# An attention block with mixture of experts: program order for the first weights and tokens, and the experts' gathers, scatters and row scalings in other slots

## The chip, the core and the metric

The kernel runs on one core of a Trainium2 chip. TensorE (PE in the profile, PEld for its weight loads) multiplies, VectorE (DVE), ScalarE (ACT) and GpSimd (POOL) do elementwise work, SyncE (SP) issues most DMAs, and POOL issues the indirect ones (gather and scatter by a list of row numbers). Every engine works through its own queue in the program's order. The metric is device time of one execution in microseconds (us); less is better. Before the change the median of three runs is 1076.01 us (1075.66 to 1076.06).

## The reference

The input is x, 2 batches of 1024 tokens with 512 features. The block is attention with a residual and a layer norm, then a mixture of experts with a residual and a layer norm:

```python
q, k, v = (lora_linear(x, W, b, Bm, Am) for each of q, k, v)   # x W^T + b + 0.5 (x Bm^T) Am^T
attn = softmax(q k^T / sqrt(32))                               # 16 heads of 32
x = layernorm(x + lora_linear(attn v, Wo, bo, Bo, Ao))
probs = softmax(x @ Wg)                                        # 8 experts, top 1
pos = position of the token in its expert's list; keep = pos < 256
h = silu(xd[e] @ W1[e]) * (xd[e] @ W3[e])                      # xd[e]: the 256 rows of expert e, H = 704
oe = h @ W2[e]
out = oe[row of the token] * gate * keep
shared = silu(x @ sw1) * (x @ sw3) @ sw2
x = layernorm(x + out + shared)
```

## The kernel before

**Precision.** A matrix operand is kept as two tiles, a rounded high part and the rest, low (wh and wl, xh and xl, hs with two halves, w13s and w2s with two halves). A product is three matmuls: high by high, low by high, high by low. ACT casts the high half, DVE or POOL subtracts to make the low half.

**The start (lines 341 to 361).** SP loads, in this order: the two LoRA factors of the Q weight, then weight chunk 0, x chunk 0, weight chunk 1, x chunk 1, up to chunk 3 (`load_w(0, ...)` with `load_xk` in its loop), then the two LoRA factors and four chunks of the K weight (`load_w(1)`). PE warms up with four matmuls on a zeroed tile (`hot`, L349). `fold_w` (L251 to L266) splits the LoRA factors and multiplies them into PSUM (`lp`, L264). For each chunk k, `split_w` adds `lp` to the raw weight (L270, DVE), casts the high part (`wh`, L271, ACT) and subtracts the low part (`wl`, L272, DVE); `split_xk` casts `xh` (L282, ACT) and subtracts `xl` (L283, POOL for the first token block); `proj_k` (L297) then runs twelve matmuls, three for each of four head groups, which need `xh` and `wh`, then `xl` and `wh`, then `xh` and `wl`. Between chunks 1 and 2 of the Q projection stands the preparation of the K weight (`prep_w(1, r1)`). In this stage PE's order is written out by hand (`manual_schedule(engines=MAN1)`, MAN1 is PE alone); the order on ACT, DVE and POOL is made by the framework's scheduler. The two memsets of L361 stand last in the code, and the scheduler puts one of them at the front of POOL's queue and one behind the four `xl`.

**Attention** follows, and then the shared expert, in eight blocks of 256 tokens. The router scatters the rows with their gate and token number into an HBM tensor by expert (`xd_d`), and the shared result plus residual goes to HBM as `bs_d`.

**The experts (lines 1090 to 1143).** One expert e has 256 rows and six slots c = 0 to 5, one for each chunk of 128 of the hidden width (chunk 5 is 64 wide). The order on PE, and from here on on ACT, DVE, POOL and SP too (MAN3 and MAN4), is the program's. A slot holds: `ffn1` (24 matmuls into one of three PSUM banks `hp`, 12 in slot 5, L829), `glu` (silu on ACT, L840, and product on DVE, L841), a load of a w13 chunk five ahead (L503), `w2_load` (L807), the high and low halves of the next expert's w13 chunk (L511 on ACT, L517 on DVE), and `split_h` (hs, L849 on ACT and L850 on DVE). The PSUM bank is free when both halves of hs are made. Beside this:

- Slot 1 of expert e holds `expert_out` of expert e - 1, for both halves of 128 rows: 17 matmuls each (`y`, L873), which take hs and w2s chunk by chunk, chunk 5 last; DVE then adds the gated result to the row's base (`be`, L1036) and takes the row statistics (L531 to L534).
- Slot 3 holds `prep_expert` of the next expert (eight transposes on PE, L413; high and low halves, L416 and L417).
- `w2_split(e, q)` makes w2s chunk q: ACT casts (L816), POOL subtracts (L817). The table `W2_AT` says in which slot: chunks 0 and 1 in slot 2, chunk 2 in slot 3, chunk 3 in slot 4, chunks 4 and 5 in slot 5. The raw tiles w2r have four buffers; the load of the tile four chunks on follows a slot after the split that frees its buffer.
- `load_base(j)` (L1023) gathers the base rows of half j from `bs_d` by an indirect DMA on POOL into a tile `be` with four buffers. Half 2e is gathered in slot 3 of expert e, half 2e + 1 in slot 5.
- For the two halves of expert e - 1: `norm_root` in slot 2 (POOL: a power, L540, and a small product, L542), `norm_rows_act` in slot 3 (ACT scales the rows, L546), `store_out` in slots 4 and 5 (POOL, indirect DMA to the output, L1040).

After expert 7 its own output, statistics, scaling and scatter close the kernel.

Of the kernel before, what the change touches and what calls it, by code (L numbers as in the profile page):

```python
# [9 lines left out]
F32 = mybir.dt.float32  # L10
# [8 lines left out]
P = 128  # L19
# [4 lines left out]
NG = 4  # L24
KC = D // P
R = 16
LR = 64 + R
LORA = 0.5
SCALE = HD ** -0.5
E, CAP, H = 8, 256, 704  # L30
# [5 lines left out]
WARM, WCOL = 4, 256  # L36
# [7 lines left out]
}  # L44
MAN1 = {mybir.EngineType.PE}
MAN2 = {
    mybir.EngineType.PE, mybir.EngineType.Activation, mybir.EngineType.DVE,
    mybir.EngineType.Pool, mybir.EngineType.SP,
# [14 lines left out]
BTB = 4  # L63
AHEAD = 5
W2_END = {2: (0, 1, 2), 3: (3, 4), 4: (5,)}
W2_AT = {2: (0, 1), 3: (2,), 4: (3,), 5: (4, 5)}
MPJ, MPP = 0, 2
RDIR = NU - 2
FINE, NRME = 2, 4
# [23 lines left out]
def kernel(  # L93
# [5 lines left out]
    def f(ap):  # L99
        return ap.bitcast(F32)  # L100
# [112 lines left out]
    with ExitStack() as ph1, tc.manual_schedule(engines=MAN1):  # L213
# [4 lines left out]
        def bank1(nm):  # L218
            if next(turn) == 3:
                return avp.tile([P, 512], F32, name=nm, tag="av")  # L220
            return one.tile([P, 512], F32, name=nm, tag="one")
# [7 lines left out]
        wl = [wp.tile([P, KC, D], F32R, name=f"wl{i}") for i in range(3)] + [wo_l]  # L229
        bv_bc = wp.tile([P, D], F32, name="bv_bc")  # L230

        def load_w(i, also=lambda k: None):
            raws = []
            for j in range(2):
                raw = next(lraw_s)[0:LR]
                sp.dma_start(out=raw, in_=lora[i, j])
                raws.append(raw)
            for k in range(KC):
                raw = next(wraw_s)
                sp.dma_start(out=raw, in_=wT[i, k])  # L240
                raws.append(raw)
                also(k)
            return raws


        def prep_w(i, raws):
            for k, lp in enumerate(fold_w(i, raws)):
                split_w(i, k, raws, lp)

        def fold_w(i, raws):  # L250
            ba = []  # L251
            for j, lo in ((0, 64), (1, 32)):
                t_ = sg.tile([LR, D], F32R, name=f"lora{i}{j}", tag=f"lora{j}", bufs=1)
                act.copy(t_, raws[j])
                rows = slice(lo, lo + R)
                dve.tensor_tensor(t_[rows], raws[j][rows], f(t_[rows]), ALU.subtract)
                ba.append(t_)
            lps = []
            for k in range(KC):
                if k == KC - 1:  # L260
                    lp = avp.tile([P, 512], F32, name=f"lp{i}{k}", tag="av")
                else:
                    lp = s1p.tile([P, 512], F32, name=f"lp{i}{k}", tag="s1")
                pe.matmul(lp, ba[0][:, k * P : k * P + P], ba[1], start=True, stop=True)  # L264
                lps.append(lp)
            return lps  # L266

        def split_w(i, k, raws, lp):
            raw = raws[2 + k]
            dve.scalar_tensor_tensor(raw, lp, LORA, raw, ALU.mult, ALU.add)  # L270
            act.copy(wh[i][:, k, :], raw)  # L271
            dve.tensor_tensor(wl[i][:, k, :], raw, f(wh[i][:, k, :]), ALU.subtract)  # L272

        def load_xk(tb, k):
            raw = next(xraw_s)
            sp.dma_start(out=raw, in_=xT[tb, k])
            return raw

        def split_xk(tb, k, raw):
            hi = sg.tile([P, 512], F32R, name=f"xh{tb}{k}", tag="xh", bufs=6)  # L280
            lo = sg.tile([P, 512], F32R, name=f"xl{tb}{k}", tag="xl", bufs=6)
            act.copy(hi, raw)  # L282
            (pool if tb == 0 else dve).tensor_tensor(lo, raw, f(hi), ALU.subtract)  # L283
            return hi, lo
# [7 lines left out]
        def proj_k(o, xs, w, g, k):  # L292
            hi, lo = xs[k]
            a = wh[w][:, k, g * P : g * P + P]
            c = wl[w][:, k, g * P : g * P + P]
            for i, (lhs, rhs) in enumerate(((a, hi), (a, lo), (c, hi))):
                pe.matmul(o, lhs, rhs, start=k + i == 0, stop=k + i == KC + 1)  # L297
# [36 lines left out]
        def pre_s1(tb):  # L334
            if tb == 3:
                for i in pre:
                    s1_step(i // 2, i % 2 * 2)
                    s1_step(i // 2, i % 2 * 2 + 1)
                    break

        x0 = []
        r0 = load_w(0, lambda k: x0.append(load_xk(0, k)))
        r1 = load_w(1)
        sp.dma_start(out=bqk_sb, in_=bqk)

        dve.memset(bo_bc, 0.0)
        for i in range(WARM):
            hot = one.tile([P, 512], F32, name=f"hot{i}", tag="one")
            pe.matmul(hot[:, 0:WCOL], bo_bc[:, 0:P], bo_bc[:, 0:WCOL], start=True, stop=True)  # L349
        lps = fold_w(0, r0)  # L350
        os_ = [bank1(f"o00{g}") for g in range(NG)]
        xs = []
        for k in range(KC):
            split_w(0, k, r0, lps[k])
            xs.append(split_xk(0, k, x0[k]))
            for g in range(NG):
                proj_k(os_[g], xs, 0, g, k)
            if k == KC - 3:
                prep_w(1, r1)
        for k_ in Ks:  # L360
            pool.memset(f(k_[96:98, :, :]), -1.0)  # L361
        for tb in range(4):
            if tb == 0:
                for g in range(NG):
# [445 lines left out]
    def w2_split(e, c):  # L810
        raw = wraw[e, 6 + c]
        if e == E - 1 and c < 2:
            hl = po["frw"].tile([P, 2, 2, 512], F32R, name=f"w2t{c}", tag="w13s", bufs=6)[:, 0]
        else:
            hl = fr.tile([P, 2, 512], F32R, name=f"w2s{e}_{c}", tag="w2s", bufs=6)
        act.copy(hl[:, 0, :], raw)  # L816
        pool.tensor_tensor(hl[:, 1, :], raw, f(hl[:, 0, :]), ALU.subtract)  # L817
        wchunk[e, 6 + c] = hl
# [202 lines left out]
    def load_base(j):  # L1021
        bases[j] = fr.tile([P, D], F32, name=f"be{j}", tag="bt", bufs=BTB)
        pool.indirect_dma_start(  # L1023
            out=bases[j],
            out_offset=None,
            in_=bs_d,
            in_offset=bass.IndirectOffsetOnAxis(ap=meta[:, j, 1:2].bitcast(I32), axis=0),
        )
# [10 lines left out]
    def store_out(j):  # L1039
        st_ = pool.indirect_dma_start(  # L1040
            out=out,
            out_offset=bass.IndirectOffsetOnAxis(ap=meta[:, j, 1:2].bitcast(I32), axis=0),
            in_=bases[j],
            in_offset=None,
        )
        st_ = st_.ins
        tc.declare_no_dep(st_, group="out", reason="different rows")
        tc.add_to_no_dep_group("out", st_)
# [41 lines left out]
    with tc.manual_schedule(engines=MAN4):  # L1090
        last = None
        for e in range(E):
            nxt = e + 1
            hss = []
            for c in range(6):
                for q in W2_END.get(c, ()) if nxt == E else ():
                    w2_split(e, q)
                hp = ffn1(e, 0, xte[e], c)
                glu(e, 0, c, hp)
                n = nxt * 6 + c  # L1100
                if n + AHEAD < E * 6:
# [12 lines left out]
                if nxt < E:  # L1114
                    w13_low(nxt, c)
                if c == 1:
                    if e:
                        for hf in range(2):
                            expert_out(e - 1, last, hf)
                    else:  # L1120
                        pend()
                if c == 3 and nxt < E:
                    prep_expert(nxt)
                if c in (3, 5):
                    load_base(2 * e + c // 2 - 1)
                for q in W2_AT.get(c, ()) if nxt < E else ():
                    w2_split(e, q)
                if e:
                    for hf in range(2):
                        j = 2 * (e - 1) + hf  # L1130
                        if c == 2:
                            norm_root(outs[j])
                        if c == 3:
                            norm_rows_act(bases[j], bases[j], outs[j])
                        if c == 4 + hf:
                            store_out(j)
            last = hss
        for hf in range(2):
            j = 2 * (E - 1) + hf
            expert_out(E - 1, last, hf)  # L1140
            norm_root(outs[j])
            norm_rows_act(bases[j], bases[j], outs[j])
            store_out(j)
# [61 lines left out]
```

## Time and profile before

| what | value |
|---|---|
| median of three runs | 1076.01 us |
| the profiled execution, its own time | 1076.59 us |
| its span, first to last instruction | 1074.9 us |
| PE busy | 1038.9 us, 97% of the span |
| DVE / ACT / POOL busy | 748.3 / 530.1 / 573.1 us |
| mean granted TensorE clock | 0.993 of full |
| data moved by DMA | 131.24 MB |

The span leaves 1.7 us of the execution's time outside. A row of a timeline has the start, the duration, engine, line, operation, what it writes and reads, and in brackets the idle time of the engine before it with what ended it; a row with x2 or more is a merged run, whose duration reaches from the first start to the last end. A row of the sums by stretch has the length, then busy time and count for PE, PEld, DVE, ACT and POOL, then the granted clock, the share of time in which the 16 DMA engines were busy, and GB/s. Ends of matmuls are modelled; starts are measured, so distances between starts are used.

### The profile page before, as it was taken

The numbers are of one execution on the slowest core, as the hardware profiler recorded it, in microseconds if no ns is written. First come the engines' busy times: TensorE is split into PE (matmuls) and PEld (weight loads), VectorE is DVE, ScalarE is ACT, GpSimd is POOL, SyncE is SP. The second block draws the span as 40 slices with busy tenths as digits, with TensorE's granted clock in tenths as the row PEclk, the third lists the DMA queues.
The fourth block names the chain that finished last, engine by engine and source line by source line (L and its number), as shares of the span: only waits on it lengthen the run. The fifth ranks groups of instructions, "written<-read, shape, count | busy, mean of one in ns | idle before, by whom it ended". The sixth has DMA issues, their size and how long they took to land. (4 is left out here: it accounts for less than half of the span.)

```text
span 1074.9 us, 16446 instructions
## 1 busy us (share of the span) xinstructions
PE 1038.9 (97%) x5992; PEld 742.9 (69%) x5992; DVE 748.3 (70%) x1217; ACT 530.1 (49%) x1026; POOL 573.1 (53%) x379
## 2 busy tenths in 40 slices
PE   8999999999999999999999999999999999999996
PEld 6888774444444455544444369889999998888885
DVE  6732788999999987799998784233522556777762
ACT  5422215666666655556666756222222455555552
POOL 5000007888888877868899575000050045666674
PEclk8999999999999999999999999999999999999999
DMA  8866860141414242042520123000082556777731
GB/s 279 288 219 202 252 195 25 52 110 48 103 47 106 71 109 70 22 90 70 119 81 22 51 60 109 20 21 20 31 240 95 161 184 207 234 234 235 237 107 59
DMA packets 77585, 131.24 MB, mean 122 GB/s; under 512 B 14344, under 2 KB 23048, under 8 KB 77504
## 3 DMA queue, kind: packets, MB, share of 16 engines
q1 hardware_dynamic: 73664, 117.59, 37.6%
q0 software_dynamic: 3840, 12.60, 3.3%
q8 instruction: 47, 0.77, 0.3%
q14 instruction: 34, 0.28, 0.1%
HBM read 96.10 MB, written 33.80 MB: 121 GB/s over the span
## 5 line engine op out<-in xcount | busy, mean ns | idle before, releaser
L588 POOL TENSOR_TENSOR pt<-pt,pt 128x1024 f32<-128x1024 f32 x151 | 360.5, 2413 | 207.7 <-ACT pt L578 190.6
L190 DVE TENSOR_REDUCE mt<-s 128x1 f32<-128x512 f32 x512 | 323.4, 680 | 39.7 <-PE s L182 39.6
L578 ACT ACTIVATE pt<-st 128x512 f32<-128x512 f32 x512 | 270.8, 602 | 141.4 <-PE st L569 137.6
L569 PE MATMUL st<-qs,ks 98*128 98x512 f32 x512 | 215.6, 432 | 1.9 <-ACT pt L578 1.2
L182 PE MATMUL s<-ks,qs 96*128 96x512 f32 x512 | 203.0, 404 | 12.7 <-DVE mt L190 11.5
L569 PEld LDWEIGHTS st<-qs,ks 98*128 98x128 f32 x512 | 96.0, 189 | 136.4 <-issue 87.2
L817 POOL TENSOR_TENSOR w2s<-w2r,w2s 128x512 fp32r<-128x512 f32 x42 | 65.7, 1582 | 127.0 <-ACT w2s L816 103.1
L829 PE MATMUL h<-xthe,w13s 128*128 128x256 f32 x704 | 131.4, 284 | 1.5 <-DVE hs L850 1.5
L182 PEld LDWEIGHTS s<-ks,qs 96*128 96x128 f32 x512 | 97.2, 190 | 41.3 <-DVE mt L190 26.8
L829 PEld LDWEIGHTS h<-xthe,w13s 128*128 128x128 f32 x704 | 111.0, 191 | 3.0 <-DVE hs L850 2.7
L829 PE MATMUL h<-xtle,w13s 128*128 128x256 f32 x352 | 100.2, 285 | 0.0
L588 DVE TENSOR_TENSOR pt<-pt,pt 128x1024 f32<-128x1024 f32 x43 | 91.4, 2131 | 3.3 <-ACT pt L578 2.9
L599 PE MATMUL av<-pt,vt 128*32 128x512 f32 x512 | 75.0, 605 | 0.0
L599 PE MATMUL av<-pt,x1b 128*32 128x512 f32 x512 | 68.8, 609 | 0.0
L829 PEld LDWEIGHTS h<-xtle,w13s 128*128 128x128 f32 x352 | 67.3, 191 | 0.7
L977 POOL DMA_INDIRECT xd_d<-x1a,slot_i x8 | 8.0, 996 | 111.8 <-DVE slot_i L974 109.7
L873 PE MATMUL y<-w2s,hs 128*128 128x512 f32 x260 | 62.7, 394 | 2.9 <-POOL w2s L817 2.9
L873 PEld LDWEIGHTS y<-w2s,hs 128*128 128x128 f32 x260 | 47.4, 188 | 15.7 <-POOL w2s L817 6.7
L297 PE MATMUL o<-xh,wh 128*128 128x512 f32 x128 | 51.1, 399 | 3.0 <-ACT wh L271 3.0
L312 ACT ACTIVATE oh<-o,bqk_sb 128x512 fp32r<-128x512 f32 x32 | 22.0, 690 | 59.0 <-PE o L297 56.5
L297 PE MATMUL o<-xl,wh 128*128 128x512 f32 x128 | 50.9, 398 | 0.0
L297 PE MATMUL o<-xh,wl 128*128 128x512 f32 x128 | 50.9, 397 | 0.0
(819 smaller groups left out, 1758.5 us busy)
## 6 DMA issues: line engine op xcount, KB each, us to landing
qs<-qkd SPq DMA_DIRECT2D x48, 256.0 KB, 5.6
ks<-qkd SPq DMA_DIRECT2D x24, 512.0 KB, 6.8
x1a<-in_w_dram SPq DMA_DIRECT2D x24, 512.0 KB, 6.8
w2r<-in_w_dram SPq DMA_DIRECT2D x42, 256.0 KB, 3.2
qkd<-oh SPq DMA_DIRECT2D x32, 256.0 KB, 2.7
qkd<-ol SPq DMA_DIRECT2D x32, 256.0 KB, 2.6
x1b<-in_w_dram SPq DMA_DIRECT2D x16, 512.0 KB, 5.7
x1b<-in_wT_dram SPq DMA_DIRECT2D x16, 256.0 KB, 5.3
```

Of the source, the lines that this page charges most:

```text
L182: pe.matmul(s1, Qs[u % 3][0:96, h, qt * P : qt * P + P], Ks[g % 2][0:96, h, kh * 512 : kh * 512 + 512], start=True, stop=True,)
L190: dve.tensor_reduce(mts[u][:, c, kh : kh + 1], s1, AX.X, ALU.max)
L297: pe.matmul(o, lhs, rhs, start=k + i == 0, stop=k + i == KC + 1)
L312: act.activation(oh, o, AF.Identity, bias=bias)
L569: pe.matmul(sb, Ks[g % 2][:, h, kc * P : kc * P + P], Qs[u % 3][:, h, :], start=True, stop=True,)
L578: act.activation(pts[t, h // 2][:, h % 2, :], sb, AF.Exp, scale=SCALE)
L588: eng.tensor_tensor(accs[u, pr], accs[u, pr], pts[t, pr], ALU.add)
L599: pe.matmul(avs[u][32 * h : 32 * h + 32, :], vts[g][:, kc, 32 * h : 32 * h + 32], pts[t, h // 2][:, h % 2, :], start=kc == 0, stop=kc == 7 ...
L817: pool.tensor_tensor(hl[:, 1, :], raw, f(hl[:, 0, :]), ALU.subtract)
L829: pe.matmul(hp[:, j * 256 : j * 256 + 256], lhs, rhs[:, k, :], start=n == 0, stop=n == 11,)
L873: pe.matmul(o, lhs, rhs, start=n == 0, stop=n == 16)
L977: sc_ = pool.indirect_dma_start(out=xd_d, out_offset=bass.IndirectOffsetOnAxis(ap=slot_i[:, i : i + 1], axis=0), in_=x1[i // 8][:, i % 8, ...
```

## The change

At the start, the loads of the K weight's LoRA factors move ahead of chunk 2 of the Q weight; the block up to the first projection is put into program order on ACT, DVE and POOL as well (`MAN0`); one more warming matmul stands on PE between the fold products and the projection; all four chunks are split before the projection's matmuls in the program (PE's order of the projection is the same); the memsets stand before and after the four splits. `prep_w` is taken apart into `split_lora`, `fold_w` for one chunk, `split_high` and `split_low`, with the same instructions. In the program that comes out, ACT's order at the start is: LoRA factors of Q (two casts), wh0, xh0, LoRA factors of K (two casts), wh1, xh1, wh2, xh2, wh3, xh3. DVE's is: fold and wl of chunk 0, fold of chunk 1, the two LoRA subtractions of K, wl of chunk 1, then fold and wl of chunks 2 and 3.

In the experts, w2s chunk 3 moves from slot 4 to slot 3 and chunk 4 from slot 5 to slot 4, and two w2r loads of each expert pass a w13 load on SP's queue. For experts 1 to 6 the two gathers move to slot 1; the scatter of the first half moves to slot 5 (ahead of w2s chunk 5), that of the second half to slot 0 of the next expert. The scaling of the rows moves to slot 4 for all experts, behind w2s chunk 4. Experts 0 and 7 keep their gathers in slots 3 and 5, expert 7 its scatters in slots 4 and 5.

```diff
+MAN0 = {mybir.EngineType.Activation, mybir.EngineType.DVE, mybir.EngineType.Pool}
...
-W2_AT = {2: (0, 1), 3: (2,), 4: (3,), 5: (4, 5)}
+W2_AT = {2: (0, 1), 3: (2, 3), 4: (4,), 5: (5,)}
...
+        def warm(nm, n):
+            for i in range(n):
+                hot = one.tile([P, 512], F32, name=f"{nm}{i}", tag="one")
+                pe.matmul(
+                    hot[:, 0:WCOL], bo_bc[:, 0:P], bo_bc[:, 0:WCOL], start=True, stop=True
+                )
+
         x0 = []
-        r0 = load_w(0, lambda k: x0.append(load_xk(0, k)))
-        r1 = load_w(1)
+        r0 = load_lora(0)
+        for k in range(KC):
+            load_wk(0, k, r0)
+            x0.append(load_xk(0, k))
+            if k == 1:
+                r1 = load_lora(1)
+        for k in range(KC):
+            load_wk(1, k, r1)
         sp.dma_start(out=bqk_sb, in_=bqk)
 
-        dve.memset(bo_bc, 0.0)
-        for i in range(WARM):
-            hot = one.tile([P, 512], F32, name=f"hot{i}", tag="one")
-            pe.matmul(hot[:, 0:WCOL], bo_bc[:, 0:P], bo_bc[:, 0:WCOL], start=True, stop=True)
-        lps = fold_w(0, r0)
-        os_ = [bank1(f"o00{g}") for g in range(NG)]
-        xs = []
+        with tc.manual_schedule(engines=MAN0):
+            dve.memset(bo_bc, 0.0)
+            warm("hot", WARM)
+            ba = split_lora(0, r0)
+            lps = [fold_w(0, ba, k) for k in range(KC)]
+            warm("warm", 1)
+            os_ = [bank1(f"o00{g}") for g in range(NG)]
+            xs = []
+
+            def split_k(k):
+                split_w(0, k, r0, lps[k])
+                xs.append(split_xk(0, k, x0[k]))
+
+            def proj_all(k):
+                for g in range(NG):
+                    proj_k(os_[g], xs, 0, g, k)
+
+            pool.memset(f(Ks[0][96:98, :, :]), -1.0)
+            for k in range(KC):
+                split_k(k)
+            pool.memset(f(Ks[1][96:98, :, :]), -1.0)
         for k in range(KC):
-            split_w(0, k, r0, lps[k])
-            xs.append(split_xk(0, k, x0[k]))
-            for g in range(NG):
-                proj_k(os_[g], xs, 0, g, k)
+            proj_all(k)
             if k == KC - 3:
                 prep_w(1, r1)
-        for k_ in Ks:
-            pool.memset(f(k_[96:98, :, :]), -1.0)
...
-                if c in (3, 5):
+                if e in (0, E - 1) and c in (3, 5):
                     load_base(2 * e + c // 2 - 1)
+                if 0 < e < E - 1 and c == 5:
+                    store_out(2 * e - 2)
                 for q in W2_AT.get(c, ()) if nxt < E else ():
                     w2_split(e, q)
+                if 0 < e < E - 1:
+                    if c == 0 and e > 1:
+                        store_out(2 * e - 3)
+                    if c == 1:
+                        load_base(2 * e)
+                        load_base(2 * e + 1)
                 if e:
                     for hf in range(2):
                         j = 2 * (e - 1) + hf
                         if c == 2:
                             norm_root(outs[j])
-                        if c == 3:
+                        if c == 4:
                             norm_rows_act(bases[j], bases[j], outs[j])
-                        if c == 4 + hf:
-                            store_out(j)
+                    if e == E - 1 and c == 0:
+                        store_out(2 * e - 3)
+                    if e == E - 1 and c > 3:
+                        store_out(2 * e - 6 + c)
```

More of the change, by code (lines that the diff above doesn't have):

```diff
@@ L230, with load_lora, load_wk, load_w @@
         bv_bc = wp.tile([P, D], F32, name="bv_bc")
-        def load_w(i, also=lambda k: None):
+        def load_lora(i):
             raws = []
             for j in range(2):
-                raw = next(lraw_s)[0:LR]
-                sp.dma_start(out=raw, in_=lora[i, j])
-                raws.append(raw)
+                raws.append(next(lraw_s)[0:LR])
+                sp.dma_start(out=raws[j], in_=lora[i, j])
+            return raws
+        def load_wk(i, k, raws):
+            raws.append(next(wraw_s))
+            sp.dma_start(out=raws[-1], in_=wT[i, k])
+        def load_w(i):
+            raws = load_lora(i)
             for k in range(KC):
[L239 to L242, printed above, removed]
+                load_wk(i, k, raws)
             return raws
         def prep_w(i, raws):
-            for k, lp in enumerate(fold_w(i, raws)):
+            ba = split_lora(i, raws)
+            for k, lp in enumerate([fold_w(i, ba, k) for k in range(KC)]):
                 split_w(i, k, raws, lp)
-        def fold_w(i, raws):
+        def split_lora(i, raws):
             ba = []
@@ L257, in fold_w, with split_high @@
                 ba.append(t_)
[L258 to L266, printed above, removed]
+            return ba
+        def fold_w(i, ba, k):
+            if k == KC - 1:
+                lp = avp.tile([P, 512], F32, name=f"lp{i}{k}", tag="av")
+            else:
+                lp = s1p.tile([P, 512], F32, name=f"lp{i}{k}", tag="s1")
+            pe.matmul(lp, ba[0][:, k * P : k * P + P], ba[1], start=True, stop=True)
+            return lp
         def split_w(i, k, raws, lp):
+            split_high(i, k, raws, lp)
+            split_low(i, k, raws)
+        def split_high(i, k, raws, lp):
             raw = raws[2 + k]
@@ L271, in split_w, with split_low @@
             act.copy(wh[i][:, k, :], raw)
+        def split_low(i, k, raws):
+            raw = raws[2 + k]
             dve.tensor_tensor(wl[i][:, k, :], raw, f(wh[i][:, k, :]), ALU.subtract)
```

## The prediction

> **What bounds the kernel now.** I read the page first: PE is busy 97% of the span, so the time is PE's work plus PE's gaps. The waits of PE, the second view, name the gaps (total us, times, longest):
>
> ```profile
> PE s L182 <- DVE mt L190: 11.5, 21, 2.2
> PE o L297 <- ACT wh L271: 3.0, 1, 3.0
> PE y L873 <- POOL w2s L817: 2.9, 6, 0.5
> ...
> PE h L829 <- DVE hs L850: 1.5, 6, 0.3
> ```
>
> The change touches none of the code behind the first row (attention), but all of the other three. The second is one gap at the start; the last two come six times each, once per expert 1 to 6. Sums over stretches that begin at chunk 2 of experts 0, 1, 2 and 3 price them (length, then PE busy):
>
> ```profile
> 867.13:891.65 24.52, 24.52 (x176) 23.12 (x174) 15.97 (x25) 13.92 (x27) 12.17 (x8) 1.00 0.75 243
> 891.65:917.51 25.86, 25.12 (x176) 23.01 (x174) 17.58 (x26) 15.33 (x29) 16.83 (x14) 1.00 0.61 194
> 917.51:943.39 25.88, 25.14 (x175) 23.02 (x174) 18.45 (x29) 15.31 (x29) 16.80 (x14) 1.00 0.74 241
> ```
>
> The first stretch holds the same 176 PE matmuls without a gap, in 24.52 us; the others take 25.86 to 25.88. A stalled expert thus loses 1.35 us, of which 0.74 is idle and the rest the slower restart. Why they stall is in the timeline of expert 2, read by engine:
>
> ```profile
> 926.18 1.57 POOL L540 TENSOR_TENSOR sce<-sce,expo 128x1 f32<-128x1 f32 x1
> ...
> 928.15 1.69 ACT L546 ACTIVATE be<-be,sce 128x512 f32<-128x512 f32 x2 [1.54 <-POOL sce L542]
> 929.74 0.36 ACT L840 ACTIVATE sl<-h 128x256 f32<-128x256 f32 x1
> ...
> 931.83 0.39 PE L829 MATMUL h<-xthe,w13s 128*128 128x256 f32 x1 [0.25 <-DVE hs L850]
> ...
> 935.55 0.97 POOL L1023 DMA_INDIRECT be<-bs_d,meta  x1 [0.30 <-issue]
> 936.55 2.53 POOL L817 TENSOR_TENSOR w2s<-w2r,w2s 128x512 fp32r<-128x512 f32 x2
> ...
> 939.13 4.42 PE L873 MATMUL y<-w2s,hs 128*128 128x512 f32 x18 [0.49 <-POOL w2s L817]
> ```
>
> ACT waits 1.54 for POOL's row roots before it scales rows (be); the silu of chunk 4 is queued behind, so chunk 4's PSUM bank is free only when PE wants it for the next expert's chunk 1. And the last two w2s halves stand on POOL behind a gather, a scatter and another gather, so y waits for the last at 939.13.
>
> At the start PE ends the fold products at 6.50 and begins the projection at 9.54:
>
> ```profile
> 8.35 0.62 ACT L282 CAST xh<-x1a 128x512 fp32r<-128x512 f32 x1 [1.70 <-DMA x1a<-in_xT_dram]
> 8.87 1.13 ACT L271 CAST wh<-x1b 128x512 fp32r<-128x512 f32 x2
> 9.54 0.80 PE L297 MATMUL o<-xh,wh 128*128 128x512 f32 x1 [3.03 <-ACT wh L271]
> ...
> 4.60:8.05 3.45, 1.63 (x6) 0.67 (x4) 2.03 (x3) 0.62 (x1) 1.99 (x3) 1.00 1.03 330
> 8.05:11.46 3.41, 1.93 (x4) 1.14 (x5) 2.40 (x4) 2.70 (x5) 1.95 (x2) 0.50 1.04 305
> 11.46:14.90 3.44, 3.44 (x10) 2.67 (x9) 3.38 (x4) 2.38 (x4) 3.19 (x3) 0.50 1.07 323
> ```
>
> Chunk 0's weight was folded by 6.52 (DVE), but its cast stands on ACT behind x chunk 1, landed at 8.3. The gap also costs clock (third column from the end): after a stretch with PE busy 1.63 of 3.45 us it is 0.50 until 14.9, and a projection matmul takes 0.43 us from start to start instead of 0.23. DMA is full here (share 1.03 to 1.07).
>
> **What the Trainium skill says.** "TensorE: Matmul & The Clock Gate", What's actually happening: the clock is halved or full by how busy PE was in windows of about 3.4 us that run free of the kernel. The trace agrees: 1.63 of 3.45 us busy lost it, a full 3.44 regained it. "SBUF — State Buffer", Who interferes with whom: a DVE instruction with two SBUF inputs and a GpSimd one that reads SBUF exclude each other. The trace agrees: the w13s subtraction that takes 1.22 us alone took 2.97 at 937.20, beside two w2s. "Perfetto Trace Analysis", DMA Instruction — SWDGE (GPSIMD): such an instruction's recorded end is the end of descriptor making, not of the transfer. Here a scatter takes 1.03 us on POOL and lands a median 4.6 us after issue.
>
> **The start.** ACT's new order is wh0, xh0, both LoRA copies of the second weight, wh1, xh1, and so on. wh0 follows the fold at 6.6, xh0 (landed 6.0) ends at 7.7, so the first matmul goes at 7.8. The second needs POOL's xl0: 1.1 to 1.3 us more, 9.1. The extra warming matmul takes 0.44 us (3.52 us for four at half clock, half of that at full) in PE's gap before 7.8 and costs nothing (0.44 to 0.88 if that gap were gone). POOL's order at the start is the same in both programs. In the stretch 4.60 to 8.05 PE is then busy 1.63 + 0.44 + 0.28 = 2.35, in the next about 2.4 of 3.41: I take it that both keep the clock. The loss is that the LoRA loads (two of 160 KB, 1.0 us at 330 GB/s) now go before x chunk 2, and wh1 waits for their copies: landing about 9.3, copies to 10.0 (DVE's two subtractions on them, 0.7 each, end by 10.9), wh1 10.5, xh1 11.1, xl1 12.2 to 12.8 (1.1 us, plus DVE's wl1 of 0.7 in the way). PE: eleven matmuls from 9.1 at 0.23, 11.6; waits until 12.7; eleven more, 15.3; four folds 0.93, 16.2; chunks 2 and 3 of 2.73 each, 21.7. Before, the same point (the K projection's first matmul) was 24.18. Gain 2.5. Were the clock half until 14.9 as before: 9.1 + 11 x 0.43 = 13.8, and 23.4 at the end, gain 0.8. Ends 0.8 to 2.9, taking 2.5. It passes through to the end if no DMA bound later holds; after 24 us PE waits for no load in the trace.
>
> **The experts, 1 to 6.** Scaling moves from slot 3 to slot 4, behind w2s 4; w2s 3 and 4 move one slot up; the gathers go to slot 1, the scatters to slots 5 and 0. SP's loads keep their kinds, two w2r loads passing a w13 load each; both wait for POOL's w2s of their buffer, which is earlier now, and each w13 chunk is loaded five slots ahead, so a us or two there is covered. In expert 2's times: silu 4 now starts when PE ends the chunk, 927.2; DVE comes free from xtle at 928.5; hs 4 is done at 929.9. Chunk 1 of expert 3 then starts at 931.4, not 931.83. POOL, free of the gather, does w2s 2 and 3 from 929.0 to 931.6 and w2s 4 (ACT's copy 929.8) to 932.8. These are back to back, so by the exclusion DVE's w13s 4, ready at 929.9, may stand until 932.8 and end at 934.0; hs 5 follows at 935.7, ACT's w2s 5 at 935.9, and POOL, which has issued the scatter by then, ends w2s 5 at 937.2 to 937.7. y starts at 934.3 and needs hs 5 at 937.7 (15 x 0.227; y's unstalled matmuls start 0.227 apart, 34 of them in 883.92 to 891.65) and the low half of w2s 5 at 937.9. Both stalls go, with only 0.2 to 0.7 us to spare in the worse order. Next comes the second scatter (to 938.9), and the gathers, which wait for the scatters to leave their buffers; behind them on POOL stands only the next w2s 0, at 947. Their data is needed a whole expert later. Gain per expert between 0.70 (a stall of 0.3 with restart left) and 1.36; I take 1.30, six times, 7.8.
>
> **The last expert.** Here the scaling, 1.52 us (1053.97 before), now sits between hs 4 (ends 1057.15) and silu 5. Before, silu 5 ran at 1057.18 and DVE's hs 5 ended 2.15 later at 1059.33; now 1058.6, and 1060.7. y starts at 1056.88 and asks for it 15 x 0.23 later, 1060.4: a new stall of 0.3, with restart 0.4 (ends 0 and 0.7).
>
> **Sum.** -2.5 - 7.8 + 0.4 = -9.9 against the profiled execution's 1076.59: 1066.7. The median of the runs is 0.58 below that execution: 1066.1.
>
> **Rivals.** (1) The clock drops at the start: windows run free, and one that spans 6.0 to 9.4 would see PE busy only about 1.5 of 3.4 us, less than what lost it before. Gain at the start 0.8 to 1.8 only: 1066.8 to 1067.8. (2) The w2s stall stays in part: DVE held off by three back-to-back w2s, hs 5 and w2s 5 later than I have them. Against it: nothing else is queued before them. Experts gain 0.7 x 6 = 4.2: 1069.7 (1068.5 to 1072). (3) Slower: the second gather waits on POOL for the scatter just issued. Scatter at 938.4, landing after 4.6 (median) to 7.9 at most, gather 1.0: POOL free at 944 to 947.3, when w2s 0 is wanted at 947.4. Each us beyond that delays w2s 5 and y by as much in five experts; it ends slower from a landing above about 10 us (9.9 / 5 = 2 us over). No scatter in this trace takes that. (4) The tail and restarts eat it all: nothing in the profile is that large.
>
> **How the numbers follow.** My forecast 0.58; rival 1 0.17; rival 2 0.19; rival 3 0.04; no visible change 0.02. About 0.2% (2.2 us) is what a measurement of this kernel can tell. Faster 0.94, same 0.02, slower 0.04. All best ends give 1076.01 - 2.9 - 8.2 = 1064.9; all worst 1071.7. The range leaves out the far part of rival 2 and rival 3: 1064.6 to 1070.8.
>
> **What would show it.** Right: o waits for POOL xl near 8 and not ACT wh at 9.5; the K projection starts near 21.7 with clock 1.00 from 4.6 on; six stretches of 24.5 to 24.6 us; no wait of h for hs nor y for w2s; the last y with a stall of 0.3 for hs. Wrong: a clock of 0.50 after 8 us, y waiting for w2s or hs in experts 1 to 6, or POOL's gather ending near the next w2s 0.

## The result and the profile after

The changed kernel takes 1068.95 us, the median of four runs (1068.41 to 1070.33), against 1076.03 us for four runs of the kernel before: a ratio of 0.9936 (95% interval 0.9919 to 0.9954), 7.1 us less. The forecast was 1066.1 us. Its direction was right, and the time lies in its range, but 2.9 us of the forecast gain are missing. The profiled execution took 1070.33 us, with a span of 1068.62.

I cut both spans at the same instructions (starts in the timelines; a score matmul is one of line 569 before and 604 after, counted from 0):

| stretch | before | after | difference | forecast |
|---|---|---|---|---|
| start to first score matmul | 158.15 | 156.69 | -1.46 | -2.5 |
| score matmul 0 to 48 | 44.16 | 47.05 | +2.89 | 0 |
| score matmul 48 to 511 | 421.65 | 421.66 | 0.0 | 0 |
| then to chunk 2 of expert 0 | 243.17 | 243.18 | 0.0 | 0 |
| chunk 2 of expert 0 to that of expert 7 | 179.69 | 171.66 | -8.03 | -7.8 |
| from there to the end | 28.06 | 28.38 | +0.32 | +0.4 |
| sum | 1074.88 | 1068.62 | -6.26 | -9.9 |

Two rows carry the miss: the start, which gave less, and a stretch of attention that no edit touches. The other forecasts hold within 0.3 us.

**The experts.** PE's waits of the kernel after (total us, times, longest) have no row left of h for hs, nor of y for w2s:

```profile
PE s L183 <- DVE mt L191: 11.9, 23, 2.2
...
PE o L310 <- POOL xl L296: 0.9, 1, 0.9
PE o L310 <- ACT xh L295: 0.8, 1, 0.8
```

The sums by stretch of the kernel after, from chunk 2 of one expert to that of the next (length, PE busy and count, PEld, DVE, ACT, POOL, clock, DMA share, GB/s):

```profile
868.58:893.10 24.52, 24.52 (x176) 23.12 (x174) 17.61 (x24) 13.92 (x27) 14.41 (x10) 1.00 0.69 229
893.10:917.62 24.52, 24.52 (x176) 23.13 (x174) 18.29 (x29) 15.34 (x29) 16.15 (x13) 1.00 0.68 228
917.62:942.14 24.52, 24.52 (x175) 23.13 (x174) 18.14 (x28) 15.34 (x29) 17.11 (x14) 1.00 0.72 248
```

Each is now as long as the one stretch that never stalled: 24.52, and not 25.88. The timeline of the kernel after in expert 2 shows what stands on POOL now, and where PE begins y:

```profile
929.05 4.80 POOL L852 TENSOR_TENSOR w2s<-w2r,w2s 128x512 fp32r<-128x512 f32 x3
...
934.41 5.84 PE L908 MATMUL y<-w2s,hs 128*128 128x512 f32 x25
...
935.41 1.31 POOL L852 TENSOR_TENSOR w2s<-w2r,w2s 128x512 fp32r<-128x512 f32 x1
...
943.89 0.96 POOL L1058 DMA_INDIRECT be<-bs_d,meta  x1 [2.58 <-DMA x1a<-in_w_dram]
```

The last low half of w2s is ready at 936.72 (935.41 + 1.31); PE, which starts y at 934.41, asks for it 16 matmuls of 0.227 us later, at 938.0. That leaves 1.3 us to spare. The second gather waits 2.58 us and ends at 944.85; the next w2s chunk starts at 947.47. The profile puts the end of that wait down to a weight load, and that of six other gathers to the landing of a scatter. Rival 3's queue is thus real, with 2.6 us of room here and 1.4 us where it is tightest, in expert 5 (995.09 to 996.51).

**The start.** Two windows of the kernel after, chosen at the place where the clock falls:

```profile
5.60:9.02 3.42, 2.04 (x7) 1.15 (x7) 1.99 (x3) 1.14 (x2) 1.03 (x1) 1.00 1.05 298
9.02:12.43 3.41, 3.11 (x7) 2.48 (x8) 2.46 (x4) 2.28 (x4) 1.05 (x2) 0.50 1.05 378
```

The first projection matmul starts at 7.96 and the second at 9.32, near the forecast 7.8 and 9.1. But the first window has PE busy for only 2.04 of 3.42 us, and the next 3.41 us run at half clock: the starts of the projection's matmuls are 0.43 us apart until 12.45 and 0.23 from there on. The K projection starts at 22.49 instead of 24.18.

**Attention.** The clock in the windows around one PE stall, first before, then after:

```profile
171.88:175.30 3.42, 1.24 (x8) 0.40 (x10) 3.39 (x5) 1.18 (x3) 2.19 (x2) 1.00 0.00 0
175.30:178.70 3.40, 3.40 (x14) 1.56 (x7) 2.08 (x5) 1.10 (x3) 3.40 (x2) 0.50 0.00 0
```

```profile
169.46:172.88 3.42, 1.45 (x7) 0.83 (x5) 3.42 (x2) 2.06 (x4) 2.19 (x2) 1.00 0.00 0
...
172.90:176.30 3.40, 3.21 (x11) 1.01 (x12) 2.12 (x5) 0.00 (x0) 3.40 (x2) 0.50 0.02 5
176.30:179.70 3.40, 3.40 (x13) 2.04 (x15) 2.26 (x4) 2.46 (x5) 2.32 (x2) 0.50 0.02 5
179.70:183.10 3.40, 3.40 (x12) 1.46 (x13) 1.06 (x2) 0.78 (x2) 3.29 (x2) 0.50 0.21 77
```

Both kernels lose the clock after a window with little PE work. The kernel before has it back after one window of 3.4 us, the kernel after only after three, 10.2 us in all. What causes the stall is the same in both. This is the timeline of the kernel after, and under it the stalled matmul of the kernel before:

```profile
164.16 7.19 POOL L623 TENSOR_TENSOR pt<-pt,pt 128x1024 f32<-128x1024 f32 x3 [143.63 <-ACT pt L613]
...
169.12 3.32 DVE L623 TENSOR_TENSOR pt<-pt,pt 128x1024 f32<-128x1024 f32 x1
...
173.09 0.79 PE L183 MATMUL s<-ks,qs 96*128 96x512 f32 x1 [2.18 <-DVE mt L191]
```

```profile
174.54 0.49 PE L182 MATMUL s<-ks,qs 96*128 96x512 f32 x1 [2.18 <-DVE mt L190]
```

POOL and DVE share the sums of the exponentials (pt). DVE's sum, 1.21 us when it runs alone, takes 3.32: the last of POOL's three sums, of 2.4 us each, begins just before it, and it ends 1.1 us after that one does. DVE's row maxima (mt), which free the PSUM banks of s, are queued behind it, and PE waits 2.18 us. In the kernel before PE waits the same 2.18 us, until 174.54. The stall was there; its price in clock was not the same. One thing does differ: in the kernel before PE resumes inside the window in which it stalled, which ends at 175.30; in the kernel after it resumes at 173.09, when the next window has begun, so that this one starts with PE idle too.

### The profile page after: what moved, and what is told of

Its sections match the earlier page's. It is cut to its first block, busy times and chain, and to the rows that moved or that the text cites. A ratio compares the mean times of both kernels' runs of the same rounds, so it can differ in the third digit from the quotient of the medians.

```text
span 1068.6 us, 16466 instructions
## 1 busy us (share of the span) xinstructions
PE 1038.4 (97%) x5994; PEld 744.8 (70%) x5994; DVE 747.8 (70%) x1217; ACT 530.4 (50%) x1026; POOL 574.7 (54%) x379
## 5 line engine op out<-in xcount | busy, mean ns | idle before, releaser
L908 PEld LDWEIGHTS y<-w2s,hs 128*128 128x128 f32 x260 | 48.2, 188 | 10.2 <-DVE hs L890 0.5
```

Source lines behind the costliest of these rows:

```text
L908: pe.matmul(o, lhs, rhs, start=n == 0, stop=n == 16)
```

## The experiments

The runs below were made on three other chips, some kernels together. On two of them (that of the parts alone and that of the repeat) every kernel, the one before too, takes some 10 us longer, so times are compared only with kernels run beside them, and stretches otherwise. On the third the kernel before was run once (1081.34 us, at a mean clock of 0.987, without a trace).

**The two parts alone.** One kernel is the one before with the experts' part of the diff (`W2_AT`, and the slots of `load_base`, `store_out` and `norm_rows_act`):

```diff
-W2_AT = {2: (0, 1), 3: (2,), 4: (3,), 5: (4, 5)}
+W2_AT = {2: (0, 1), 3: (2, 3), 4: (4,), 5: (5,)}
...
+                if 0 < e < E - 1 and c == 5:
+                    store_out(2 * e - 2)
...
+                    if c == 1:
+                        load_base(2 * e)
+                        load_base(2 * e + 1)
...
-                        if c == 3:
+                        if c == 4:
                             norm_rows_act(bases[j], bases[j], outs[j])
```

The other is the kernel after with these lines as they were before:

```diff
-W2_AT = {2: (0, 1), 3: (2, 3), 4: (4,), 5: (5,)}
+W2_AT = {2: (0, 1), 3: (2,), 4: (3,), 5: (4, 5)}
...
-                if e in (0, E - 1) and c in (3, 5):
+                if c in (3, 5):
                     load_base(2 * e + c // 2 - 1)
...
-                        if c == 4:
+                        if c == 3:
                             norm_rows_act(bases[j], bases[j], outs[j])
...
+                        if c == 4 + hf:
+                            store_out(j)
```

Expected of the experts alone:

> The kernel before with the experts' part of the change alone. Both theories: six experts of 24.5 us instead of 25.86, the two waits of PE (h for hs, y for w2s) gone, the last expert 0.3 us longer; 1076.0 - 8.0 + 0.3 = 1068.3 us. If the experts' slots also changed anything ahead of them (they should not), the point where expert 0 begins its slot 2 would not be at 867 us.

Expected of the start alone:

> The kernel before with the start's part alone. Theory A (the start gains 1.7 us, and the clock then takes it back near 175 us by chance of where its windows lie): the K projection's first matmul at 22.5 us instead of 24.2, attention's first score matmul 1.5 us earlier, then as many us lost again as windows at half clock exceed the one of before, 1.7 us each: between 1074.4 (one window) and 1077.4 us (three windows). Theory B (loads or DVE take the start's gain back in the projections, whatever the clock): the first score matmul no earlier than before, 1076 us.

Measured beside the kernel before (1088.20 us): experts alone 1082.82 us, ratio 0.9942 (0.9925 to 0.9960); start alone 1088.29 us, 0.9996 (0.9983 to 1.0009). The experts' part holds all of the gain that can be told from none; the start's interval still holds a gain of up to 0.17%, 1.8 us. Its seven pitches are 24.51 to 24.53 us, and its end is 28.40. In the run of the start alone, the K projection starts at 23.57, not at 22.49. Its sums by stretch show why:

```profile
4.60:8.00 3.40, 2.21 (x9) 1.23 (x7) 2.10 (x5) 1.14 (x2) 0.94 (x3) 1.00 0.96 307
8.00:11.40 3.40, 2.70 (x6) 1.85 (x7) 2.16 (x4) 2.28 (x4) 1.12 (x1) 0.50 1.05 340
11.40:14.80 3.40, 3.40 (x9) 2.67 (x8) 2.37 (x4) 1.45 (x3) 2.43 (x2) 0.50 1.07 371
```

The window 4.60 to 8.00 is the one that the prediction spoke of. PE was busy in 2.21 us of it (forecast 2.35), which was not enough; two windows at half clock followed. The experts alone, whose attention is that of the kernel before up to there, had 10.2 us of half clock between 161.8 and 182.3 (one window from 161.8, two from 175.5) and took 46.88 us from score matmul 0 to 48; the start alone had 3.4 and took 44.14. So the 2.9 us do not go with the start's edits.

**The sums shared out otherwise.** DVE's second sum of unit 0, the one that is late, goes to POOL, in the kernel after and in the kernel before:

```diff
-                eng = dve if (kc, pr) in DVE_END.get(u, ON_DVE) else pool
+                eng = dve if (kc, pr) in DVE_END.get(u, ON_DVE if u else ON_DVE[:1]) else pool
```

> The changed kernel with one more edit: in attention's first unit the sum of exponentials at step 2, pair 1, is made by POOL instead of DVE. Theory A: DVE no longer stands 2.1 us behind POOL there, so PE's stall of 2.18 us is gone, the clock stays full from 12.4 us to the last expert, and the score matmul of step 6 comes near 176.5 us instead of 183.2; end 1062 to 1064 us, and the runs lie closer together than the 1068.4 to 1070.3 of the changed kernel. Theory B (the loss between 150 and 185 us is a wait on DVE or POOL and not the clock): the stall moves to a later POOL sum, clock unaffected; 1067 to 1069 us.

> The kernel before with the same edit of attention's first unit. Theory A: the one half-clock window at 175.3 us and the stall go, 4.2 us by the distance between the score matmuls of steps 4 and 6: 1071.8 us. Theory B: at most the stall itself, 2.2 us: 1073.8 to 1076 us.

The expectation that this removes the stall failed. The kernel after with this edit took 1084.73 us (ratio to the kernel before 0.9960, 0.9948 to 0.9972), which is 1.9 us more than the experts' part alone, a difference that their intervals don't settle; the kernel before with it took 1092.39 (1.0031, 1.0019 to 1.0043), slower. The stall moves to the next unit and grows. Timeline of the kernel after with this edit:

```profile
177.99 11.74 POOL L623 TENSOR_TENSOR pt<-pt,pt 128x1024 f32<-128x1024 f32 x5
...
187.87 6.46 DVE L623 TENSOR_TENSOR pt<-pt,pt 128x1024 f32<-128x1024 f32 x1
...
189.69 1.25 POOL L709 TENSOR_TENSOR x1a<-x1a,bo_bc 128x512 f32<-128x512 f32 x1
190.92 2.33 POOL L623 TENSOR_TENSOR pt<-pt,pt 128x1024 f32<-128x1024 f32 x1
...
194.99 0.80 PE L183 MATMUL s<-ks,qs 96*128 96x512 f32 x1 [5.50 <-DVE mt L191]
```

DVE's sum now takes 6.46 us: it waits through the last sum of POOL's run and two more POOL instructions behind it, and PE waits 5.50. More work on POOL made a longer wait on DVE and PE, as a chain from POOL's sums over DVE to PE would have it; the cure was wrong. The run also gave the one start at full clock throughout: K projection at 22.19.

**The same kernel again, and with the stall filled.** The kernel after unchanged, the kernel after with five dummy matmuls (`fill`, each the same as a warming matmul) where PE stalls:

```diff
+            if t == 4:
+                between[1].append(lambda: fill(5))
```

> The changed kernel once more, for the phase of the clock's windows. Theory A (where the half-clock windows fall is chance): its profile shows another set of them than 9.0 to 12.4 and 172.9 to 183.1 us, with the six experts again at 24.5 us each; the K projection's first matmul between 21.7 and 23.6 us, the stretch from attention's score matmul 16 to 48 between 29.4 us (no half clock) and 33.7 us (10.2 us of it). Theory B (the change itself makes the long stretch at half clock near 175 us): 10 us of half clock there again.

> The changed kernel with five warming matmuls (0.44 us each, their result is not used) in PE's gap of 2.18 us near 171 us, ahead of the matmul that waits for DVE. Theory A (the idle gap costs the clock, and the clock the time): no half-clock window between 13 us and the shared expert, score matmuls 16 to 48 in 29.2 to 29.8 us instead of 30.8 to 33.7, so 1.3 to 4.3 us faster than the changed kernel. Theory B (the clock falls there for another reason, or falls without costing time): half clock near 175 us as before, the same time or slower by the extra matmuls.

The repeat took 1079.30 us (ratio 0.9932, 0.9909 to 0.9956, the same as on the first chip within the intervals), with one window of 3.4 us at half clock in attention instead of three. The same program thus has both; the 10.2 us were not made by the change. Its K projection started at 23.43.

Where the stall ends beside the window goes with what it costs. The stalled matmul of the repeat, then that of the experts alone with the window behind its stall:

```profile
174.18 0.50 PE L183 MATMUL s<-ks,qs 96*128 96x512 f32 x1 [2.19 <-DVE mt L191]
```

```profile
175.80 0.79 PE L182 MATMUL s<-ks,qs 96*128 96x512 f32 x1 [2.30 <-DVE mt L190]
...
175.47:178.88 3.41, 3.08 (x10) 0.98 (x11) 2.25 (x5) 0.00 (x0) 3.41 (x2) 0.50 0.00 0
```

In the repeat the window ends at 174.65, after PE has resumed. Nine profiled executions have this stall without a fill. In seven of them PE resumes 0.4 to 1.0 us before the end of the window in which it stalled, and half clock lasts one window. In the other two, the kernel after and the experts alone, it resumes 0.2 and 0.3 us into the next window, and half clock lasts three windows and two. All nine fit the windows' phase as the cause; no run moved the stall to test it.

With the fill: 1078.32 us (0.9924, 0.9896 to 0.9952), 1.0 us below the repeat by medians (1.3 to 4.3 were expected), which their ranges (1077.42 to 1080.01 and 1077.91 to 1081.56) don't settle. Its timeline has the dummy matmuls in the gap:

```profile
171.71 2.35 PE L620 MATMUL fill<-bo_bc 128*128 128x256 f32 x10
```

In that run no half clock follows, nor in the one of the candidate below, which has the fill too; all nine without it have some. Score matmuls 0 to 48 take 42.82 us in both. With 44.16 for 3.4 us of half clock (before) and 47.05 for 10.2 (after), one us at half clock costs 0.39 to 0.41 us here: (44.16 - 42.82) / 3.4 and (47.05 - 42.82) / 10.2. At these rates the two extra windows (6.8 us) of the profiled execution are worth 2.7 to 2.8 of the +2.89.

**What each experts' edit is worth.** The scaling alone moved to slot 4 in the kernel before, and all of the change but that:

```diff
-                        if c == 3:
+                        if c == 4:
                             norm_rows_act(bases[j], bases[j], outs[j])
```

> The kernel before with the row scaling alone moved to slot 4. The wait of h for hs goes in experts 1 to 6. If POOL's queue (gather, scatter, gather ahead of the last w2s) is what y waits for, the last w2s ends when it did, y starts 0.5 us earlier and waits as much longer: experts stay at 25.6 to 25.9 us. If the late silu was behind both waits, they fall to 24.5 us.

> The kernel after, with the scaling of the rows put back to slot 3 (gathers, scatters and w2s chunks stay where the change has them). Theory A (the two waits are separate: the scaling in slot 4 takes away h's wait for hs, the gathers, scatters and w2s chunks take away y's wait for w2s): h's wait for hs is back six times at 0.2 to 0.3 us, y's wait for w2s stays away, pitch of the stalled experts 24.9 to 25.2 us, and the last part of the kernel is 28.06 again instead of 28.38. Theory B (the scaling only stalls where POOL is late, and POOL is no longer late): pitch 24.5. Theory C (the scaling's move was the whole gain): pitch 25.8.

The scaling alone (one run, 1083.05 us, beside 1085.57 for the kernel before) gave 25.02 to 25.06 us from one expert to the next in five of the six stalled experts and 25.47 in the first; the gathers, scatters and w2s chunks alone gave 25.00 to 25.03 in all six. So the first gains 4.48 us in six experts and the second 5.04, where both together gain 8.03. Neither of the two values expected of the scaling alone, 25.6 to 25.9 or 24.5, came out; theory A of the other run did. PE's waits, first with the scaling alone, then with all but the scaling:

```profile
PE y L873 <- POOL w2s L817: 1.7, 6, 0.5
```

```profile
PE h L864 <- DVE hs L885: 1.5, 6, 0.3
```

The scaling takes away h's wait and shortens y's from 0.49 to about 0.24 us in five experts ((1.7 - 0.5) / 5), most likely because ACT and DVE, without the first stall, reach the next chunk earlier, and with them y's last inputs; this was not tried by itself. The other edits take away y's wait and leave h's as it was. Either stall that is left costs about 0.25 us of idle PE and as much again in restart (25.02 - 24.52). With the scaling in slot 3 the last part of the kernel is 28.06 us again, so the 0.32 at the end is the scaling's.

**The start's small edits.** Without the one more warming matmul; and with K's LoRA loads behind x chunk 3 again:

```diff
-            warm("warm", 1)
```

```diff
-            if k == 1:
-                r1 = load_lora(1)
+        r1 = load_lora(1)
```

> The kernel after, without the one more warming matmul. Theory A (it costs nothing and helps only where a window happens to sit on the edge): first projection matmul at 7.8 to 8.4, the K projection's first matmul at 23.4 to 23.7 with 6.8 us of half clock from about 8 on, as in those runs of the change's start that kept half clock so long. Theory B (it matters for nothing): 22.2 to 22.5 with 3.4 us of half clock or none. One run can tell a value below 22.6 from A, but a value of 23.5 fits both, since the same start with the warming matmul has given 22.2 to 23.6.

> The kernel after, with the loads of the K weight's LoRA factors back behind x chunk 3. Theory A (the early LoRA loads delay chunk 1 but let the K weight be folded between the chunks): chunks 1 and 2 no longer wait for the loads, but ACT's and DVE's queues stand in program order on LoRA factors that land at about 14, so chunk 2's projection starts later than in the kernel after (17.0 for its first matmul, 13.4 for the fold before it), and the K projection's first matmul is at 23.5 to 25. Theory B (the order of loads does not matter because PE's own work is the bound from 9.3 on): 22.2 to 23.7, as in the kernel after.

The K projection started at 23.56 without the matmul and at 23.70 with the late loads; one run each, 1068.49 and 1068.70 us, on the chip of the run with the scaling in slot 3 (1070.74). The second lies in the ranges of both theories and decides nothing; the run with the fill, whose half clock at the start ended at the same time (14.5), had 23.58, so that the order of loads looks worth about 0.1 us at most there. The first decides nothing, as the expectation said: the change's own start gave 23.41 to 23.58 in four runs and less in two. These two runs are useful for another reason: with 3.4 us of half clock in attention, their spans are 1066.8 and 1067.0.

**A candidate.** The fill, the scaling of expert 7 in slot 3, and for chunks 0 and 1 of the first projection all high-by-high products first, then high by low, then low by high, which asks for xl last:

```diff
-                for g in range(NG):
+                hi, lo = xs[k]
+                for i in (0, 2, 1) if k < 2 else ():
+                    for g in range(NG):
+                        pe.matmul(
+                            os_[g], (wl if i == 2 else wh)[0][:, k, g * P : g * P + P],
+                            lo if i == 1 else hi, start=k + i == 0, stop=False,
+                        )
+                for g in range(NG) if k > 1 else ():
                     proj_k(os_[g], xs, 0, g, k)
...
-                        if c == 4:
+                        if c == (4 if nxt < E else 3):
```

> The changed kernel with those five matmuls, with expert 7's row scaling back in slot 3, and with the first two chunks of the Q projection in another order (for all four head groups first high by high, then high by the weight's low half, then low by high). The last y loses its wait for hs: 0.3 us. The start: PE no longer waits for POOL's xl, K projection's first matmul at 20.7 us at full clock, 21.5 if one window falls, instead of 22.2 to 23.6: about 1.5 us. With the clock kept near 175 us: 3 to 6 us faster than the changed kernel.

It took 1076.72 us (1075.97 to 1077.53), a ratio of 0.9905 (0.9879 to 0.9931) to the kernel before; the repeat of the kernel after beside it took 1077.91 to 1081.56, so it beats both, the latter by 2.6 us of medians where 3 to 6 were expected. Its range touches that of the kernel with the fill alone (1077.42 to 1080.01). The end is 28.06 us, as expected. At the start the order did its work, chunk 2's projection starting at 16.74 instead of 17.02, but the K projection came at 23.66, not in the expected 20.7 to 21.5. Its timeline names what stands there instead:

```profile
23.66 0.50 PE L310 MATMUL o<-xh,wh 128*128 128x512 f32 x1 [1.30 <-DVE ol L326]
```

PE now waits for DVE, which must read the first projection's PSUM bank (ol) and does it late, behind the splits of the weights. PE being ready earlier brings nothing at this point. Which of the splits or loads before it sets DVE's time was not tried.

## Why the prediction was right or wrong

- **The experts: right.** Forecast 6 x 1.30 = 7.8, measured 8.03: 1.34 per expert, near the best end of 0.70 to 1.36. That DVE's w13s would stand through the w2s run was too dark: the w13s at 929.74 took 1.69 us, with an end at 931.4 instead of 934.0. The slack at y was 1.3 us, more than the forecast 0.2 to 0.7. The forecast 0.74 idle and the rest restart stands; the parts show that each stall costs as much again as its idle time.
- **The tail: right.** Forecast +0.4, measured +0.32. The chain that ended last has y waiting for the hs that stands behind the scaling.
- **The start: the step that failed is "I take it that both keep the clock".** The size of the start was taken with full clock. The trace of the run shows 2.04 us busy in the window 5.60 to 9.02, and half clock for the next; this is rival 1, by its own mechanism. It left the K projection 1.69 earlier instead of 2.5, of which 1.46 reach attention. And the usual outcome is worse. Over the runs of the change's start with all its edits, the K projection starts at 22.19 (no half clock), 22.49 (one window), and 23.41, 23.43, 23.57 and 23.58 (matmuls 0.43 apart until about 14). With the kernel before's start it was 23.55, 24.00, 24.02 and 24.18. The usual gain is about 0.5 us by medians. At equal clock it is 0.1 to 0.6: 23.55 became 23.41 where half clock ended at 14.1, and 24.18 became 23.57 where it ended at 14.9 and 14.8. That is under the low end of 0.8, whose 23.4 ("were the clock half until 14.9") is what the traces show. Even at full clock it was 22.19 and not 21.7. The second chunk's xl was ready at 13.0, forecast 12.7; and the K projection's first matmul then waited for DVE's `ol`, which ended at 22.14. It came 0.41 after the matmul before it instead of 0.23. This is the bound that the candidate met too, and the prediction had no term for it:

```profile
22.19 0.19 PEld L310 LDWEIGHTS o<-xh,wh 128*128 128x128 f32 x1 [0.44 <-DVE ol L326]
```

- **Attention: a term that was not in the sum.** "It passes through to the end if no DMA bound later holds" named the wrong condition. The rest of the kernel was taken to run at the clock of the profile before. One stall that both kernels have cost 3.4 us of half clock in one and 10.2 in the other, +2.89 us. The repeat of the same program shows that this is not the change's doing.
- **The sum.** In the profiled execution, start +1.04, attention +2.89, experts -0.23 and tail -0.08 against the forecast make the 3.6 us by which -6.26 misses -9.9. For the median, 2.85 us over the forecast, only the profiled one of the four runs has a trace. The two late runs of the start's variants, with one window in attention, lie 1.8 and 2.0 us above the forecast span (1074.88 - 9.9 = 1064.98). So about 2 of the 2.85 are the start's size, and the rest is most likely windows at half clock, which was not shown for those runs; that their mean clock rises as the time falls (0.991, 0.992, 0.992 and 0.995 for 1070.33 to 1068.41 us) fits it. That the time still lies in the forecast range is owed to the experts, which came out near their best end, and to the room that the range left for rival 1; the loss in attention was in no part of it.
- **Rival 2** did not happen: no wait of y for w2s is left. **Rival 3** did not either, with 1.4 us of room in the tightest expert. **Rival 4**, restarts and tail, was 0.32 us.

"TensorE: Matmul & The Clock Gate", What's actually happening, in the Trainium skill, tells that windows of activity decide the clock, and every trace here agrees on their length of about 3.4 us: the recorded stretches at half clock before the kernel's end last 3.41 us or two, three or four times that. It does not tell which amount of busy time keeps the clock, and neither do the traces. These two windows, of the experts alone and of the candidate, were followed by half clock and by full clock:

```profile
158.40:161.81 3.41, 2.35 (x9) 1.19 (x9) 3.41 (x7) 2.46 (x5) 0.00 (x0) 1.00 0.20 77
```

```profile
21.13:24.54 3.41, 2.11 (x10) 1.44 (x9) 3.35 (x6) 3.18 (x7) 0.77 (x1) 1.00 0.29 111
```

The three windows of the full-clock start, from 4.4, had PE busy for 2.1 to 2.7 us and kept it; 2.04 and 2.21 us lost it elsewhere. So the profile's busy time alone does not decide it.

## What to carry to other kernels

Two small stalls in a loop that are one behind the other on different engines are priced together: of the 8.03 us that both edits gave in six experts, one alone gave 4.48 and the other 5.04. A gain at the start that needs the full clock should be counted at half clock, and the full-clock value kept as the far end, unless PE is busy through every possible window there. And before an edit is credited with a few us, look at the granted clock in stretches that it does not touch: the half clock after one unchanged stall cost 1.3 us in one execution and 4.2 in another.

## What the hardware did that I had not expected

- **The clock came back late.** After the stall in attention, half clock lasted 3.4 or 10.2 us for the same program, although the windows 172.90 to 176.30 and 176.30 to 179.70 have PE busy for 3.21 and 3.40 of 3.40 us. Where the stall lies fits part of this: in the kernel after it reached into the window from 172.85. Over all thirteen profiled executions 26 windows at half clock have PE busy for 3.3 us or more, and 25 of them were followed by full clock; the window 176.30 to 179.70 is the one that was not. What decides it there stays open.
- **DVE can wait for more than one POOL instruction.** "SBUF — State Buffer", Who interferes with whom, in the Trainium skill, says that a DVE instruction with two SBUF inputs contends with a GpSimd one that reads SBUF, and, of DVE's two-port modes, that the first to issue keeps the shared ports for its whole instruction while the other is blocked. Here a DVE sum of 1.21 us took 3.32 behind the rest of one POOL sum, which fits that, and 6.46 behind the rest of one and two more: it did not get in between them. But in the kernel after the subtraction w13s, 1.22 us alone, came in behind the first of three w2s (1.31 us), and the second w2s stretched to 2.28 us (929.05 + 3.54 is 932.59; the second begins at 930.31):

```profile
929.05 3.54 POOL L852 TENSOR_TENSOR w2s<-w2r,w2s 128x512 fp32r<-128x512 f32 x2
929.74 1.69 DVE L552 TENSOR_TENSOR w13s<-x1a,w13s 128x1024 fp32r<-128x1024 f32 x1
```

Which of the two comes about, and why, was not tried.

- **PE stood still with no wait on record.** On the two slower chips PE has idle times near 790 us, while the router's scatters run, for which the profile names no wait but "issue" (the engine waited for nothing that the profile shows), here of the start alone:

```profile
PE y-1_4_0_7932 L908 <- issue: 5.4, 5, 1.6
```

With the half clock that follows (10.2 us from 793.1 in this run), these are probably most of what the kernels lose there: the stretch from the last score matmul to chunk 2 of expert 0 took 254.15 us in this run and 243.17 on the first chip. The traces of the first and third chip have no such row. Why it is so on some chips was not tried.
